# A quantile stage on selection networks: min and max in place with one operand copied to PSUM, two tiles in turn, five gather buffers

## The chip, the cores and the metric

The kernel runs on one core of a Trainium2 chip. The metric is the device time of one execution in microseconds, as the median over several runs. A profiled execution gives, beside its own time, a record of each instruction; engine names are PE (TensorE), PEld (its weight loads), DVE (VectorE), ACT (ScalarE), POOL (GpSimd) and SP (SyncE).

## The reference

Two layers follow each other on a graph of 4096 nodes with 128 features; about 32 neighbours a node.

```python
# layer 0: graph attention, 8 heads
e = leaky_relu(f1[:, :, None] + f2[:, None, :], 0.2)      # f1, f2: nodes @ W[h] @ a1[h], a2[h]
att = softmax(where(adj > 0, e, -9e15), axis=-1)
h = elu(einsum('hnm,hmd->hnd', att, Wh))
x = layernorm(nodes + elu(cat(h) @ W1 + b1)) * gamma + beta
# layer 1: quantiles over the kept neighbours, per feature
rank = cumsum(mask, axis=1) - 1
keep = mask & ~((rank + 1) % skip[:, None] == 0)          # skip = ceil(neighbours / 2), or 1
svals = sort(where(keep[:, :, None], x[None], big), axis=1)
agg = mean of svals at ceil(q * n_keep) - 1 for q in (0.25, 0.5, 0.75)   # 0 with nothing kept
out = (0.5 * agg + 0.5 * x) @ W.T + b + x
```

So each node needs, for each of 128 features, three order statistics over some 10 to 60 values that lie in rows of the first layer's output.

## The kernel before, in words

**Tiles.** 128 nodes make a tile (one node a partition), 32 tiles in all. The nodes are sorted by their number of neighbours (rank_by_count, L593), so that tile t holds nodes with at most CAP[t] neighbours and its list of kept neighbours has 2 * HT[t] slots: 22 in the smallest tile, 42 in the second largest, 62 in the largest (LMAX); 1022 slots in all tiles.

**Attention.** neighbours (L476) finds each node's neighbour list from the adjacency rows, in three blocks of 2, 8 and 22 tiles. The loop at L344 works through each block: it scatters the records (list, number, own index, attention terms, features) into a DRAM table in sorted order, and then takes a step (L311) for each tile. A step fetches the tile's record (fetch_rows, L685: tile R, six buffers, loaded by four DMAs on SP's queue; POOL then gathers one neighbour of each node per indirect DMA into G), writes the finished x1 rows of an earlier pair of tiles with scatter (L168, on POOL; it reads its row numbers from R, so R is held until then), weighs the tile before (weigh_rows, L746) and starts transform (L833) for each pair of tiles. In the first two blocks the order on DVE, PE and ACT is the order of the text (manual_schedule); in the last block a scheduler orders the instructions. In the last block 32 further scatters write list, number and own index of all nodes into all_d, spread over the 22 steps.

**The seam.** After the last step kept_rows (L962) loads all_d and makes, tile by tile with six small DVE instructions each, the slot lists idx; it also counts nodes that the fast way can't take (bad, total). Pads stand in for missing slots: rows of -BIG and BIG in x1_d.

**Quantiles.** The loop at L402 goes over the tiles, small ones first, large ones in the middle. fetch_list (L389) issues one indirect DMA for each slot (gather, L159, on POOL: 128 rows of 512 bytes from x1_d into vals[:, j, :]) and one for the node's own row, xs. vals has two buffers. slot_weights (L1005) makes the weight of each slot in the mean, five small DVE instructions a tile. quantile_out (L1029) runs the selection network (selection_network, L84): 15 or 21 stages a tile. In a stage of distance d the lower of slots i and i + d goes to slot i (mins) and the higher to slot i + d (maxs), where either is needed later. groups (L110) turns the slots of a stage into strided pieces, one DVE tensor_tensor each (L1037), reading the buffer of the stage before and writing the other of two work buffers; slots that no pair touches are copied across by ACT (L1044). Then three to fourteen slots are summed with their weights (L1050), PE transposes the sum (L1056) and multiplies it with the layer's weights (L1060), and DVE adds xb (L1062); POOL scatters the tile to the output (L403, through L168). [...] The scheduler puts the instructions of this stage in order.

## Time and profile before

| | us |
|---|---|
| three runs | 4443.7, 4440.7, 4423.36 |
| median | 4440.7 |
| the profiled execution's own time | 4429.16 |
| its span, first to last instruction | 4427.4 |
| busy: DVE, POOL, ACT, PE | 2559.9, 2815.6, 902.0, 881.4 |
| last gather of the attention stage starts | 2407.0 |
| last x1 rows scattered | 2455.0 |
| first gather of a list, first min of a network | 2458.1, 2509.9 |
| last gather of a list | 4381.5 |
| last DVE instruction (o, L1062) | 4421.6 |

The profile's page gives busy time for each engine, and in 40 equal slices of the span its share in tenths (one slice is 110.7 us). A row of a group reads: line, engine, operation, output<-inputs by name, shapes, count | busy us in all, mean ns of one | idle us of the engine just before them, and what ended the idle time ("issue" is time in which the engine waited for nothing that the profile shows). A row in order of time reads: start us, length us, engine, line, operation, names, shapes, count, and the idle time before it. In the rows names are shortened: x_d is x1_d, xt_d the table of node rows.

### The profile page before, as it was taken

What the parts mean: (1) busy time and instruction counts of PE and PEld (TensorE: products, weight loads), DVE (VectorE), ACT (ScalarE), POOL (GpSimd) and SP (SyncE); (2) the same over time, 40 slices, a digit from 0 to 9 for tenths busy, and PEclk for the clock granted to TensorE, in tenths of its full rate; (3) what the DMA queues carried; (4) which work ended last, traced back from release to release, by engine and by line L of the source; (5) the groups of instructions that cost most, each with busy time, mean ns of one, the idle gap of its engine ahead of it and who ended that gap; (6) DMA issues with size and microseconds to landing.
All of it is one profiled execution on the core that took longest, in us unless ns stands there. A gap on an engine that the chain in (4) does not pass through costs nothing. (4 is left out here: it accounts for less than half of the span.)

```text
span 4427.4 us, 19351 instructions
## 1 busy us (share of the span) xinstructions
PE 881.4 (20%) x4003; PEld 459.4 (10%) x4009; DVE 2559.9 (58%) x5054; ACT 902.0 (20%) x1210; POOL 2815.6 (64%) x2399
## 2 busy tenths in 40 slices
PE   4323444433123332323323000000000000000000
PEld 2000211211122211212212000000000000000000
DVE  5554555555312111112112489987788898779998
ACT  2101212111001110001101022213443223441223
POOL 2432343344566666666664658888888888888885
PEclk9955655556556555555555555555555555555555
DMA  5313233221111111111112101111111101111110
GB/s 169 107 47 114 97 94 102 93 91 44 47 48 48 48 45 48 48 49 49 49 47 56 41 28 40 38 39 41 38 37 33 30 27 33 38 39 38 38 40 29
DMA packets 116271, 242.31 MB, mean 55 GB/s; under 512 B 51920, under 2 KB 69328, under 8 KB 107952
## 3 DMA queue, kind: packets, MB, share of 16 engines
q0 software_dynamic: 76224, 161.01, 13.2%
q10 hardware_dynamic: 12160, 68.49, 4.4%
q1 hardware_dynamic: 27760, 11.49, 1.2%
q14 instruction: 94, 0.77, 0.1%
q8 instruction: 33, 0.54, 0.0%
HBM read 229.64 MB, written 11.18 MB: 54 GB/s over the span
## 5 line engine op out<-in xcount | busy, mean ns | idle before, releaser
L159 POOL DMA_INDIRECT vals<-x_d,idx x1022 | 1474.7, 1443 | 314.1 <-issue 303.1
L1037 DVE TENSOR_TENSOR work<-work 128x256 f32<-128x256 f32 (+12 forms) x1331 | 1497.7, 1170 | 163.0 <-ACT work L1044 126.9
L159 POOL DMA_INDIRECT G<-xt_d,idx x1092 | 1058.1, 969 | 797.0 <-issue 394.6
L1044 ACT COPY work<-work 128x512 f32<-128x512 f32 (+12 forms) x671 | 529.5, 830 | 1102.8 <-DVE work L1037 974.1
L518 DVE MAX8 first<-key 128x8 f32<-128x128 f32 x1024 | 224.3, 286 | 326.6 <-remote 200.3
L1056 PE MATMUL st_ps<-ident,s 128*128 128x128 f32 x32 | 15.2, 474 | 1914.9 <-DVE s L1050 1573.1
L777 PE MATMUL y<-G,pf 128*32 128x129 f32 (+2 forms) x2224 | 219.5, 382 | 454.2 <-issue 345.4
L846 DVE TENSOR_SCALAR e<-e 128x512 f32<-128x512 f32 x64 | 27.7, 433 | 438.5 <-issue 246.1
L512 PE MATMUL key<-sgn,markb 128*128 128x512 bf16 x252 | 146.5, 581 | 531.1 <-DVE first L518 357.5
L798 DVE TENSOR_SCALAR rden<-y 128x6 f32<-128x6 f32 x64 | 7.3, 153 | 354.2 <-remote 179.2
L1056 PEld LDWEIGHTS st_ps<-ident,s 128*128 128x128 f32 x32 | 5.8, 181 | 1924.5 <-DVE s L1050 1581.3
L826 ACT COPY yT<-turned 128x512 f32<-128x512 f32 x64 | 65.5, 1023 | 651.8 <-PE turned L825 335.2
L491 ACT ACTIVATE sgn<-adj_t 128x2048 bf16<-128x2048 int32 x64 | 121.9, 1905 | 372.5 <-PE key L512 174.6
L777 PEld LDWEIGHTS y<-G,pf 128*32 128x32 f32 (+2 forms) x2224 | 138.1, 162 | 539.8 <-issue 408.0
L865 PE MATMUL hT<-yT,W_sb 128*128 128x256 f32 x256 | 119.3, 605 | 276.1 <-DVE hv L848 105.9
L873 ACT ACTIVATE e<-hT 128x512 f32<-128x512 f32 x64 | 38.2, 596 | 610.7 <-remote 438.1
L168 POOL DMA_INDIRECT x_d<-x,R x32 | 32.5, 1016 | 201.4 <-DVE x L912 148.0
L514 PE MATMUL key<-parts,oneb 64*128 64x512 bf16 x256 | 147.4, 576 | 3.2 <-issue 3.2
L168 POOL DMA_INDIRECT rec_d<-rec,ranks x32 | 32.2, 1005 | 159.3 <-issue 123.9
L525 DVE MAX8 rec<-first 128x8 f32<-128x256 f32 x256 | 109.4, 427 | 41.5 <-remote 27.6
L765 DVE TENSOR_TENSOR pf<-z,own 128x1024 f32<-128x1024 f32 x62 | 75.3, 1219 | 94.1 <-ACT z L761 40.5
L1037 DVE TENSOR_TENSOR work<-vals 128x1536 f32<-128x1536 f32 (+8 forms) x64 | 94.9, 1483 | 49.3 <-DMA vals<-x_d,idx 49.0
(171 smaller groups left out, 1674.5 us busy)
## 6 DMA issues: line engine op xcount, KB each, us to landing
adj_t<-in_adj_dram ACTq DMA_DIRECT2D x64, 1024.0 KB
G<-xt_d,idx POOLq DMA_INDIRECT x1092
vals<-x_d,idx POOLq DMA_INDIRECT x1022
R<-rec_d SPq DMA_DIRECT2D x128, 26.4 KB
xt_d<-rec SPq DMA_DIRECT2D x4, 548.0 KB
score<-rec_d SPq DMA_DIRECT2D x132, 1.0 KB
rec<-in_x_dram SPq DMA_DIRECT2D x4, 512.0 KB
Gs<-xt_d,idx POOLq DMA_INDIRECT x92
```

The lines of the kernel that those rows point to most:

```text
L159: nc.gpsimd.indirect_dma_start(out=dst, out_offset=None, in_=rows, in_offset=bass.IndirectOffsetOnAxis(ap=idx, axis=0),)
L491: nc.scalar.activation(sgn, adj_t, AF.Sign, accum_out=cnt[:, i : i + 1])
L512: nc.tensor.matmul(key, lhsT=markb, rhs=sgn[:, ts(b, 512)], start=True, stop=False)
L514: nc.tensor.matmul(key, lhsT=oneb[0:64, :], rhs=parts[:, c0 : c0 + 512], start=False, stop=True)
L518: nc.vector.max(first[:, ts(c0 // CW + c, 8)], key[:, ts(c, CW)])
L525: nc.vector.max(top, first)
L765: nc.vector.tensor_tensor(pf.rearrange("p (g k h) -> p g k h", g=w, k=k), z.unsqueeze(2).to_broadcast(spread), own[w].unsqueeze(1).unsquee ...
L777: nc.tensor.matmul(block(b)[p0 : p0 + m, :], lhsT=pf[:, c : c + m], rhs=G[:, g, 0 : D + 1], start=(i == 0 and b % 3 == 0), stop=last, skip ...
L826: nc.scalar.copy(yT[:, :, ts(place, P)].rearrange("p h (u g) -> p g u h", u=4)[:, ts(half, 16)], t_ps.rearrange("p b (g u h) -> p (b g) u ...
L865: nc.tensor.matmul(hT[:, ts(j, n)], lhsT=consts["W_sb"][:, h, :], rhs=yT[:, h, 0:n], start=True, stop=True,)
L1037: nc.vector.tensor_tensor(slots_of(nxt, (b + low, k, stride, m)), slots_of(cur, (b, k, stride, m)), slots_of(cur, (b + d, k, stride, m)), op,)
L1044: nc.scalar.copy(slots_of(nxt, g), slots_of(cur, g))
```

## The change

It has five parts.

1. **In place, one operand in PSUM.** The work buffers go. A stage splits its slots into three kinds: both ends needed, only the lower, only the higher. Each kind's pieces are cut to at most TURN = 12 slots (pieces_of). For each piece ACT copies the lower slots to a PSUM tile (low, two buffers of 12 * 128 values), and DVE then writes min into the lower and max into the higher slots of vals itself, reading the copy and the higher slots. Pieces of under four slots with only one end are done without a copy. Slots that no pair touches stay where they are.
2. **Two tiles in turn.** quantile_out is a generator that yields after each stage and each step of the end; the loop runs two of them in turn. The order on DVE, PE, ACT and POOL in this part is that of the text.
3. **Five gather buffers.** vals has five buffers of LMOST = 42 slots; the one tile of 62 slots has a buffer of its own (most). Five lists are fetched ahead; when a tile is done its result is scattered, the next list is fetched, and the next tile begins.
4. **Lists and weights for eight tiles at a time.** kept_rows makes its lists with instructions over eight tiles and 62 slots; limits (LOW, CAP, HT for each tile) is filled by POOL at the start. It and slot_places move into step 11 of the last attention block; for that, the 32 scatters to all_d go out four a step in the first eight steps. slot_weights is made the same way, ahead of the quantile loop. Counting bad nodes is now count_bad, after the last step.
5. **Record buffers.** R in fetch_rows has five buffers in place of six.

```diff
--- before.py
+++ after.py
@@ -16,6 +16,7 @@
 PSUM = bass.MemoryType.PSUM
 DRAM = bass.MemoryType.DRAM
 ORDERED = {mybir.EngineType.DVE, mybir.EngineType.PE, mybir.EngineType.Activation}
+ALL = ORDERED | {mybir.EngineType.Pool}
 
 P = 128
 N = 4096
@@ -60,6 +61,8 @@
 ]
 HT = [(c - 1) // 2 for c in CAP]
 LMAX = 2 * max(HT)
+LMOST = 2 * sorted(HT)[-2]
+TURN = 12
 
 
 R_NUM, R_OWN, R_F1 = L, L + 1, L + 2
@@ -127,6 +130,29 @@
                 j += 1
         out.append((b, j - i, stride, n))
         i = j
+    return out
+
+
+def pieces_of(g):
+
+
+    b, k, stride, n = g
+    if k == 1:
+        parts = -(-n // TURN)
+        out = []
+        for i in range(parts):
+            m = (n - sum(p[3] for p in out)) // (parts - i)
+            out.append((b, 1, m, m))
+            b += m
+        return out
+    if n >= TURN:
+        return [p for i in range(k) for p in pieces_of((b + i * stride, 1, n, n))]
+    parts = -(-k // (TURN // n))
+    out = []
+    for i in range(parts):
+        kk = (k - sum(p[1] for p in out)) // (parts - i)
+        out.append((b, kk, stride, n))
+        b += kk * stride
     return out
 
 
@@ -262,6 +288,12 @@
         narrow.append(sets)
     idx = const.tile([P, NT, L], I32, name="idx")
     own_i = const.tile([P, NT], I32, name="own_i")
+    picks = const.tile([P, 4, NT], F32, name="picks")
+    limits = const.tile([P, 3, NT], F32, name="limits")
+    for i, values in enumerate((LOW, CAP, HT)):
+        for t, v in enumerate(values):
+            if t == 0 or v != values[t - 1]:
+                nc.gpsimd.memset(limits[:, i, t:], float(v))
 
 
     rp = tc.alloc_tile_pool(name="recp", bufs=1)
@@ -353,10 +385,17 @@
             adjp.release()
             cp = tc.alloc_tile_pool(name="cnt_all", bufs=2, side="right", reuse_waits="tile")
             ranks = rank_by_count(tc, cp, kp, num, jp1, before, oneb, 0, NT)
+            waiting = list(range(NT))
             for i in range(n):
                 step((recs_d[b], i, CAPS[n][i], t0 + i))
-                for t in range(i * NT // n, (i + 1) * NT // n):
+                for t in waiting[:4]:
                     scatter(nc, all_d, rec[:, t, 0:REC1], ranks[:, t : t + 1])
+                waiting = waiting[4:]
+                if i == n // 2:
+                    R = cp.tile([P, NT, REC1], F32, name="R", bufs=1)
+                    nc.sync.dma_start(R, all_d.rearrange("(t p) w -> p t w", p=P))
+                    kept_rows(tc, cp, R, jp1, pidx, idx, own_i, bad, limits)
+                    slot_places(tc, cp, R, picks, limits)
         else:
             pieces = search(t0 + n, BLOCKS[b + 1])
             quota = -(-BLOCKS[b + 1] * PIECES // n)
@@ -368,9 +407,7 @@
         t0 += n
     for _ in range(3):
         step()
-    R = cp.tile([P, NT, REC1], F32, name="R", bufs=1)
-    nc.sync.dma_start(R, all_d.rearrange("(t p) w -> p t w", p=P))
-    kept_rows(tc, cp, kp, R, jp1, pidx, ones, idx, own_i, bad, total)
+    count_bad(tc, cp, kp, bad, ones, total)
     cp.release()
     attp.release()
     rp.release()
@@ -380,38 +417,51 @@
 
     order = sorted(range(NT), key=lambda t: HT[t])
     order = order[0::2] + order[1::2][::-1]
-    with tc.tile_pool(name="late", bufs=1) as lp, tc.tile_pool(name="sort", bufs=2) as sp, tc.tile_pool(
+    with tc.tile_pool(name="late", bufs=1) as late, tc.tile_pool(name="sort", bufs=5) as sp, tc.tile_pool(
         name="fin", bufs=3
-    ) as fp, tc.tile_pool(name="fin_ps", bufs=2, space=PSUM) as pp:
-        lists = []
-        outs = []
-
-        def fetch_list(t):
-            vals = sp.tile([P, LMAX, D], F32, name="vals")
-            for j in range(2 * HT[t]):
+    ) as fp, tc.tile_pool(name="low_ps", bufs=2, space=PSUM) as lp, tc.tile_pool(
+        name="fin_ps", bufs=1, space=PSUM
+    ) as pp, tc.manual_schedule(engines=ALL):
+        wt = late.tile([P, NT, LMAX], F32, name="wt")
+        slot_weights(tc, late, jp1, picks, wt)
+        waiting = list(order)
+        lists, running, outs = [], [], []
+
+        def fetch_list():
+            t = waiting.pop(0)
+            n = 2 * HT[t]
+            if n > LMOST:
+                vals = sp.tile([P, LMAX, D], F32, name="most", bufs=1)
+            else:
+                vals = sp.tile([P, LMOST, D], F32, name="vals")
+            for j in range(n):
                 gather(nc, vals[:, j, :], x1_d, idx[:, t, j : j + 1])
-            xs = fp.tile([P, D], F32, name="xs")
+            xs = fp.tile([P, D], F32, name="xs", bufs=6)
             gather(nc, xs, x1_d, own_i[:, t : t + 1])
             lists.append((t, vals, xs))
 
-        def write_out():
-            t, o = outs.pop(0)
-            scatter(nc, out, o, own_i[:, t : t + 1])
-
-        wt = lp.tile([P, NT, L], F32, name="wt")
-        for t in order:
-            fetch_list(t)
-            if t == order[0]:
-                R = lp.tile([P, NT, REC1], F32, name="R")
-                nc.sync.dma_start(R, all_d.rearrange("(t p) w -> p t w", p=P))
-                slot_weights(tc, lp, R, jp1, wt)
-            if len(outs) > 1:
-                write_out()
-            if len(lists) > 1:
-                outs.append(quantile_out(tc, sp, fp, pp, *lists.pop(0), wt, ident, WlT, vecs[:, 3, :]))
-        outs.append(quantile_out(tc, sp, fp, pp, *lists.pop(0), wt, ident, WlT, vecs[:, 3, :]))
-        while outs:
-            write_out()
+        def begin():
+            if lists:
+                running.append(
+                    quantile_out(
+                        tc, lp, fp, pp, *lists.pop(0), wt, ident, WlT, vecs[:, 3, :], outs
+                    )
+                )
+
+        for _ in range(5):
+            fetch_list()
+        begin()
+        begin()
+        while running:
+            for g in list(running):
+                if next(g, True):
+                    running.remove(g)
+                    while outs:
+                        t, o = outs.pop(0)
+                        scatter(nc, out, o, own_i[:, t : t + 1])
+                    if waiting:
+                        fetch_list()
+                    begin()
 
 
     flag = nc.values_load(total[0:1, 0:1], min_val=0, max_val=1 << 20)
@@ -686,7 +736,7 @@
 
     nc = tc.nc
 
-    R = ap.tile([P, REC], F32, name="R", bufs=6)
+    R = ap.tile([P, REC], F32, name="R", bufs=5)
     rows = rec_d[ts(i, P), :]
     for u, v in enumerate(rows.rearrange("(g u) w -> u g w", u=4)[k] for k in range(4)):
         nc.sync.dma_start(R[ts(u, 32), :], v)
@@ -959,21 +1009,9 @@
     return keeps, h
 
 
...
+def count_bad(tc, cp, pp, bad, ones, total):
+
+    nc = tc.nc
     t_ps = pp.tile([P, 512], F32, name="key")
     nb = bad.rearrange("p a t -> p (a t)")
     nc.tensor.matmul(t_ps[0:1, 0 : 5 * NT], lhsT=ones[:, 0:1], rhs=nb, start=True, stop=True)
@@ -981,86 +1019,130 @@
     nc.vector.tensor_reduce(tot, t_ps[0:1, 0 : 5 * NT], AX.X, ALU.add)
     nc.vector.tensor_copy(total, tot)
 
+
+def kept_rows(tc, cp, R, jp1, pidx, idx, own_i, bad, limits):
+
+
+    nc = tc.nc
+    num = R[:, :, R_NUM]
+    nc.vector.tensor_copy(own_i, R.bitcast(I32)[:, :, R_OWN])
+    keeps, h = kept_halves(tc, cp, num, NT)
+    few = cp.tile([P, NT], F32, name="few")
+    nc.vector.tensor_tensor(few, num, limits[:, 0, :], ALU.is_lt)
+    nc.vector.tensor_tensor(few, few, keeps, ALU.mult)
+    many = cp.tile([P, NT], F32, name="many")
+    nc.vector.tensor_tensor(many, num, limits[:, 1, :], ALU.is_gt)
+    nc.vector.tensor_tensor(bad[:, 1, :], few, many, ALU.add)
+
     nk = cp.tile([P, NT], F32, name="nk")
     nc.vector.tensor_scalar(nk, h, 2.0, None, ALU.mult)
+    top = cp.tile([P, NT], F32, name="top")
+    nc.vector.tensor_tensor(top, h, limits[:, 2, :], ALU.add)
     padrow = cp.tile([P, 1], F32, name="padrow")
     nc.vector.tensor_scalar(padrow, pidx, float(N), None, ALU.add)
...
+    m = 8
+    big = [P, m, LMAX]
+    jb = jp1[:, 0:LMAX].unsqueeze(1).to_broadcast(big)
+    for t0 in range(0, NT, m):
+        here = slice(t0, t0 + m)
+        pad = cp.tile(big, F32, name="pad", bufs=1)
+        nc.vector.tensor_tensor(pad, jb, top[:, here].unsqueeze(2).to_broadcast(big), ALU.is_gt)
+        nc.vector.tensor_scalar(pad, pad, float(P), padrow, ALU.mult, ALU.add)
+
+        d = cp.tile(big, F32, name="d", bufs=1)
+        nc.vector.tensor_tensor(d, R.bitcast(I32)[:, here, 0:LMAX], pad, ALU.subtract)
+        own = cp.tile(big, F32, name="held", bufs=1)
+        nc.vector.tensor_tensor(own, jb, nk[:, here].unsqueeze(2).to_broadcast(big), ALU.is_le)
+        nc.vector.tensor_tensor(d, d, own, ALU.mult)
+        nc.vector.tensor_tensor(idx[:, here, 0:LMAX], d, pad, ALU.add)
+
+
+def slot_places(tc, pool, R, picks, limits):
 
     nc = tc.nc
     keeps, h = kept_halves(tc, pool, R[:, :, R_NUM], NT)
     nk = pool.tile([P, NT], F32, name="nk")
     nc.vector.tensor_scalar(nk, h, 2.0, None, ALU.mult)
...
+    nc.vector.tensor_scalar(picks[:, 3, :], keeps, 1.0 / 6.0, None, ALU.mult)
     for q in range(3):
...
+        k = picks[:, q, :]
         nc.vector.tensor_tensor(k, places(tc, pool, nk, q + 1), h, ALU.subtract)
...
+        nc.vector.tensor_tensor(k, k, limits[:, 2, :], ALU.add)
+
+
+def slot_weights(tc, pool, jp1, picks, wt):
+
+    nc = tc.nc
+    m = 8
+    big = [P, m, LMAX]
+    jb = jp1[:, 0:LMAX].unsqueeze(1).to_broadcast(big)
+    hit = pool.tile(big, F32, name="hit")
+    for t0 in range(0, NT, m):
+        here = slice(t0, t0 + m)
+        w = wt[:, here, :]
+        for q in range(3):
+            nc.vector.tensor_tensor(
+                hit if q else w,
+                jb,
+                picks[:, q, here].unsqueeze(2).to_broadcast(big),
+                ALU.is_equal,
+            )
+            if q:
+                nc.vector.tensor_tensor(w, w, hit, ALU.add)
+        nc.vector.tensor_tensor(
+            w, w, picks[:, 3, here].unsqueeze(2).to_broadcast(big), ALU.mult
+        )
+
+
+def quantile_out(tc, lp, fp, pp, t, vals, xs, wt, ident, WlT, bl_b, outs):
+
 
     nc = tc.nc
     targets = sorted(quantile_slots(t))
...
+    for d, mins, maxs, _ in selection_network(2 * HT[t], targets):
+        lows, highs = set(mins), set(maxs)
+        kinds = (
+            (sorted(lows & highs), (0, d)),
+            (sorted(lows - highs), (0,)),
+            (sorted(highs - lows), (d,)),
+        )
+        for slots, ends in kinds:
+            for g in (p for whole in groups(slots) for p in pieces_of(whole)):
+                b, k, stride, m = g
+                low, high = slots_of(vals, g), slots_of(vals, (b + d, k, stride, m))
+                if k * m >= 4 or len(ends) == 2:
+                    kept = lp.tile([P, TURN * D], F32, name="low")[:, 0 : k * m * D]
+                    if k > 1:
+                        kept = kept.rearrange("p (k d) -> p k d", k=k)
+                    nc.scalar.copy(kept, low)
+                else:
+                    kept = low
+                for end in ends:
+                    nc.vector.tensor_tensor(
+                        high if end else low, kept, high, ALU.max if end else ALU.min
+                    )
+        yield
 
     s = fp.tile([P, D], F32, name="s")
     nc.scalar.mul(s, xs, 0.5)
+    xb = fp.tile([P, D], F32, name="xb")
+    nc.vector.tensor_tensor(xb, xs, bl_b, ALU.add)
     for j in targets:
         nc.vector.scalar_tensor_tensor(
...
+            s, vals[:, j, :], wt[:, t, j : j + 1], s, ALU.mult, ALU.add
+        )
+    yield
     st_ps = pp.tile([P, P], F32, name="st_ps")
     nc.tensor.transpose(st_ps, s, ident)
     sT = fp.tile([P, P], F32, name="sT")
     nc.scalar.copy(sT, st_ps)
+    yield
     o_ps = pp.tile([P, D], F32, name="fo_ps")
     nc.tensor.matmul(o_ps, lhsT=sT, rhs=WlT, start=True, stop=True)
+    yield
     o = fp.tile([P, D], F32, name="o")
     nc.vector.tensor_tensor(o, o_ps, xb, ALU.add)
...
+    outs.append((t, o))
 
 
 def general_attention(tc, x, adj, wa, x1_d, f2T_d, consts):
```

Where lines are left out, they are the lines of kept_rows, slot_weights and quantile_out that stand in the kernel before.

## The prediction

> **What bounds the kernel now.** I read the page's slices first, then the sums over four stretches of the last stage, then the groups, then single instructions in order of time. From slice 23 on there is only one stage left, the quantile stage, and in it two engines are nearly full:
>
> ```profile
> DVE  5554555555312111112112489987788898779998
> ...
> POOL 2432343344566666666664658888888888888885
> ```
>
> The sums over stretches give, for each engine, busy us and the number of instructions (the order is PE, PEld, DVE, ACT, POOL):
>
> ```profile
> 2600.00:4380.00 1780.00, 36.78 (x87) 19.75 (x87) 1568.86 (x1595) 558.34 (x711) 1475.46 (x1000) 0.50 0.13 37
> ```
>
> POOL issues 1000 indirect DMAs in 1780 us. Each has 0.30 us of issue ahead of it (see the gather rows below), so POOL is taken for 1475 + 300 = 1775 of 1780 us. VectorE is busy for 1569, 88%. So POOL's gathers set the pace here, at 1.78 us each, and VectorE is second. The groups and the gather's spread:
>
> ```profile
> L159 POOL DMA_INDIRECT vals<-x_d,idx x1022 | 1474.7, 1443 | 314.1 <-issue 303.1
> L1037 DVE TENSOR_TENSOR work<-work 128x256 f32<-128x256 f32 (+12 forms) x1331 | 1497.7, 1170 | 163.0 <-ACT work L1044 126.9
> L159 POOL DMA_INDIRECT G<-xt_d,idx x1092 | 1058.1, 969 | 797.0 <-issue 394.6
> ```
>
> ```profile
> L159 POOL DMA_INDIRECT vals<-x_d,idx x1022: 938/1356/4030, 2458.1 to 4381.5; - x171
> ```
>
> The same instruction with rows of the same size takes 969 ns in the attention stage and 1443 here, between 938 and 4030. In order of time it is seen why: it is short while VectorE stands still, and grows while VectorE runs min and max.
>
> ```profile
> 3061.23 0.94 POOL L159 DMA_INDIRECT vals<-x_d,idx  x1 [0.30 <-issue]
> 3062.47 0.94 POOL L159 DMA_INDIRECT vals<-x_d,idx  x1 [0.30 <-issue]
> 3063.71 9.40 DVE L1037 TENSOR_TENSOR work<-work 128x1280 f32<-128x1280 f32 x5 [2.74 <-ACT work L1044]
> ...
> 3067.77 1.83 POOL L159 DMA_INDIRECT vals<-x_d,idx  x1 [0.30 <-DMA vals<-x_d,idx]
> 3069.90 1.63 POOL L159 DMA_INDIRECT vals<-x_d,idx  x1 [0.30 <-issue]
> ...
> 3071.83 2.09 POOL L159 DMA_INDIRECT vals<-x_d,idx  x1 [0.30 <-issue]
> ```
>
> [...] 0.94 us beside an idle VectorE, 1.6 to 2.1 us beside min and max. [...] 692 ns with a PSUM input, 688 without. [...]
>
> ```profile
> L848 DVE TENSOR_TENSOR hv<-hT,e 128x512 f32<-128x512 f32 x8 | 5.5, 692 | 0.4
> L1037 DVE TENSOR_TENSOR work<-work 128x512 f32<-128x512 f32 x88 | 58.6, 688 | 3.5 <-ACT work L1044 1.6
> L1037 DVE TENSOR_TENSOR work<-work 128x2048 f32<-128x2048 f32 x144 | 325.3, 2289 | 33.7 <-ACT work L1044 24.7 <-issue 2.4 <-DVE s L1050 1.5
> L1044 ACT COPY work<-work 128x1024 f32<-128x1024 f32 x124 | 128.2, 1044 | 214.6 <-DVE work L1037 201.5 <-DVE s L1050 7.2 <-issue 4.8
> ```
>
> **The change, part by part.** *Min and max in place.* I counted by evaluating the code's own plan of the network (selection_network, groups, pieces_of) for the 32 tiles. Before: 552 stages, 1395 min and max instructions (the page's 1331 + 64) over 10,766 slots, and 699 ScalarE copies. After: the same 10,766 slots, but in pieces of at most 12 slots: 1823 instructions, of which 348 (675 slots) have both inputs in SBUF because they are not worth a copy; and 761 copies of 5149 slots. From 512 and 2048 elements, an instruction is 0.157 us + 1.042 ns an element. 10,766 x 128 elements are 1436 us either way; the fixed part grows from 219 to 286 us. So 1722 us instead of 1655. But instructions overlap: 1331 x 1.170 = 1557 us of durations fill 1498 us. Where nothing is waited for, a 1.22 us instruction is followed after 1.14 us (2596.09, next at 2597.23), so 0.083 less. A third of them do wait now, mostly for the stage before on the same tile. With two tiles taken stage by stage in turn that stage lies a whole stage back, so I take the overlap for all: 1722 - 1823 x 0.083 = 1571 us.
>
> *Copies to PSUM.* From 512 (616 ns) and 1024 (1044): 0.19 us + 0.836 ns an element, 761 copies = 694 us. They lie beside VectorE, which has 1571. With two PSUM buffers a copy can start when the piece two back has been used. I walked the pieces in program order with these durations and 0.1 us to pass a finished piece on. VectorE then stands still for 60 us in all, nearly all where a small piece is followed by one of 12 slots (a copy of 1.47 us against about 0.5 us of min and max). If the cover of the second tile were gone, the same walk gives 270.
>
> *POOL.* 1022 + 32 + 32 issues x (0.94 + 0.30) = 1347 us. A few grow beside the 348 SBUF pairs and the 140 weighted sums; at 1.30 + 0.10 each it is still 1520. POOL then is no longer the bound. Five buffers let it stay up to three tiles ahead; a finished tile's scatter stands in POOL's order before the next list, and the lists behind it are then already there.
>
> *Weighted sums and the rest.* 140 x 0.377 (four took 1.51 us) = 53 us, now in a row without other work between; xb and o, 64 x 0.2 = 13 us.
>
> *Lists and weights eight tiles at a time.* The 288 small instructions of the lists and the 160 of the weights go; the lists move into step 11 of the last block, where VectorE is under 20% busy. There the 24 wide ones cost 24 x 0.67 = 16 us, plus one 1 MB load on SP's queue ahead of later record loads (the same load takes 11 us today); both lie under some 57 us a tile of POOL time. The weights (24 instructions, 16 us) run while the first lists arrive. What is saved at the seam: little. The last transform's chain ran on through the list work, and the first gather waited for the scatter:
>
> ```profile
> 2450.98 0.96 POOL L168 DMA_INDIRECT x_d<-x,R  x1 [37.68 <-DVE pad L994]
> 2455.05 0.95 POOL L168 DMA_INDIRECT x_d<-x,R  x1 [3.11 <-DVE d L998]
> 2458.13 0.97 POOL L159 DMA_INDIRECT vals<-x_d,idx  x1 [2.13 <-DMA x_d<-x,R]
> ```
>
> I take 5 us, so the first gather at 2453. The 55 memsets of limits at the start are POOL work of 0.1 us beside a load that is waited for anyway: 0.
>
> *Record buffers, six to five.* A record tile is freed by its scatter, and the load follows it at once, 66 us ahead of its use:
>
> ```profile
> 2051.89 1.00 POOL L168 DMA_INDIRECT x_d<-x,R  x1 [0.30 <-issue]
> 2054.16 15.01 SPq L692 DMA_DIRECT2D R<-rec_d  x8
> ```
>
> That is about one tile of POOL time. With one buffer less every second tile loses that lead, and then scatter, load and transpose (some 7 us) stand open in POOL's order, ahead of all later gathers: 16 x 7 = 112 us at the worst. POOL already waits 105 us for PE's y in this stretch, and the two waits may fall together: 0 at best, I take 25.
>
> **Sum, against the profiled execution (span 4427.4, time 4429.2).** First gather 2453; first list 23 x 1.24 + 2.1 = 31 us; the second tile's list 31 us more, of which 2 are used: VectorE is fed from 2513. Then 1571 + 53 + 13 + 60 = 1697 → 4210; last transposes 3, scatter and end 6 → 4219; records 25 → 4244, time 4246. That is 0.9586 of 4429.2. The median of before is 4440.7, 0.3% higher than the profiled one; on it, **4257 us**. VectorE is what is late next: the stage ends with it 97% full.
>
> **Rivals.**
> 1. *VectorE is not so dense.* The overlap is lost where the max writes what the min has just read[...]: 714 pairs x 0.18 = 130[...] us. About 4340 to 4400, still faster. For it: a third of today's instructions start 20 to 120 ns late. Against: independent ones don't. 20%.
> 2. [...] POOL stays the bound at 1.78 us: 2453 + 1086 x 1.78 = 4386, the last list's work 35, end 6: 4427, about 4440 on the median. No change. Against: rows 3061 to 3072. 7%.
> 3. *Slower: copy and min/max take turns.* In place, a copy reads the tile that VectorE is writing. If the order is kept for whole spans of the tile and not for the slots, each copy waits for the min and max of the piece before, and VectorE for each copy: 694 us + 761 x 0.12 = 785 us on VectorE. Then 4244 + 725 = 4970. It decides from about 230 of the 761 copies exposed. Against: a copy of ten slots of vals ran at 2480, with the first tile's gathers still coming (23 issues from 2458), so slots are told apart. 7%.
>
> **Chances.** My forecast, 4200 to 4340, has 66%. A measurement tells this kernel from no change at about 0.5%. Faster by more: 66 + 20 = 86%; within 0.5%: 7%; slower: 7%. Range 4195 to 4400, below for a tighter handshake and no loss on records, above for rival 1 with both its costs.
>
> **What would show it.** Right: gathers of vals near 0.95 us, POOL idle between lists, VectorE over 95% busy from 2515 on with some 1820 min and max, ScalarE's copies near 690 us. Wrong: gathers still at 1.4 us (rival 2); VectorE waiting for ScalarE's copies for hundreds of us (rival 3); VectorE at durations over 0.157 us + 1.04 ns an element, or starts later than the end before (rival 1); POOL waiting for record loads in the attention stage (records over 25 us).

## The result, and the profile after

The changed kernel takes 4567.0 us (median of 4 runs, 4564.2 to 4572.5) beside 4434.2 for the kernel before (a fourth run, 4427.6, joined the three with the median 4440.7): ratio 1.030, 95% interval 1.027 to 1.033. Forecast were 4257 us, 0.959. The change is slower by 3.0%.

Runs come in rounds, each with its own runs of the kernel before, and since these took 4408 to 4438 us (medians) in the round of the result and those of the first eleven experiments but 3943 to 3944 in the later ones, each ratio is taken within its round.

First the slices of the changed kernel's page, then its groups, then the tile view of the list buffers (duration min/median/max in ns, first and last start).

```profile
DVE  5554466546031122211111156888897999999998
...
POOL 2433434443765555555654476566576342445640
```

```profile
L185 POOL DMA_INDIRECT G<-xt_d,idx x1092 | 1050.8, 962 | 955.7 <-issue 505.4
L1121 DVE TENSOR_TENSOR vals<-low,vals 128x1024 f32<-128x1024 f32 (+10 forms) x1359 | 1390.2, 1056 | 211.7 <-remote 65.6
L185 POOL DMA_INDIRECT vals<-x_d,idx x960 | 907.1, 945 | 294.4 <-issue 283.1
...
L827 PE MATMUL y<-G,pf 128*32 128x129 f32 (+2 forms) x2224 | 216.3, 369 | 836.1 <-issue 691.3
...
L194 POOL DMA_INDIRECT out_dram<-o,own_i x32 | 31.8, 993 | 617.5 <-DVE o L1144 607.3
```

```profile
L185 POOL DMA_INDIRECT vals<-x_d,idx x960: 940/944/1213, 2593.5 to 4427.0; - x192
```

What the change is meant to do, it does: list gathers fall from 1443 to 945 ns, and POOL, full in this stage before, now waits 607 us for VectorE's outputs. Yet the first list gather starts at 2593.5 instead of 2458.1, and from there to the end it takes 1970.9 us (4564.4 less 2593.5) where it took 1969.3. So there are two losses to explain: 135 us ahead of the stage that was rebuilt, and a gain inside that stage that didn't come.

Two other lines stand out beside those of before. TensorE's wait ahead of the y matmuls, put down to "issue" (nothing in the trace was waited for), is 691 us; before it was 345. And 66 us of VectorE's waits ahead of min and max are named "remote" (a release from nowhere in the trace). The kernel before has such waits too, but nearly all ahead of its quantile stage; of its page:

```profile
L777 PE MATMUL y<-G,pf 128*32 128x129 f32 (+2 forms) x2224 | 219.5, 382 | 454.2 <-issue 345.4
L798 DVE TENSOR_SCALAR rden<-y 128x6 f32<-128x6 f32 x64 | 7.3, 153 | 354.2 <-remote 179.2
```

Both waits belong together, as two stretches of the changed kernel in order of time show. First the attention stage:

```profile
2129.74 1.00 POOL L194 DMA_INDIRECT x_d<-x,R  x1 [0.30 <-issue]
2132.07 8.51 SPq L742 DMA_DIRECT2D R<-rec_d  x8
...
2133.61 0.38 PE L827 MATMUL y<-G,pf 128*32 128x129 f32 x1 [2.42 <-issue]
2135.01 0.13 PEld L827 LDWEIGHTS y<-G,pf 128*32 128x32 f32 x1 [2.67 <-issue]
...
2148.02 0.23 DVE L848 TENSOR_SCALAR rden<-y 128x6 f32<-128x6 f32 x2 [64.45 <-PE y L827]
...
2168.59 0.14 DVE L756 TENSOR_SCALAR bad<-R 128x1 f32<-128x1 f32 x1
...
2168.94 0.20 DVE L771 STREAM_TRANSPOSE idx<-list 128x32 int32<-128x32 int32 x1
...
2169.63 0.97 POOL L185 DMA_INDIRECT G<-xt_d,idx  x1 [36.37 <-PE y L827]
```

The scatter frees a record buffer, and the load follows at 2132. VectorE first touches the new record at 2168.59: its order has the last tile's rden, yn and transform ahead of it, and these stood 64 us behind matmuls that TensorE started one in 2.8 us. POOL can't form the next gathers until then: the trace puts its wait down to y, but the first gather starts 0.49 us after VectorE has transposed the row numbers (idx), here as at four other long pauses of POOL. Now the quantile stage:

```profile
3443.04 0.28 DVE L1121 TENSOR_TENSOR vals<-low,vals 128x128 f32<-128x128 f32 x1
...
3443.63 0.27 ACT L1117 COPY low<-vals 128x128 f32<-128x128 f32 x1 [5.33 <-DVE vals L1121]
...
3451.33 0.29 DVE L1121 TENSOR_TENSOR vals<-low,vals 128x128 f32<-128x128 f32 x1 [8.01 <-remote]
```

The copy is over at 3443.90, its reader starts 7.4 us later, and in between POOL issues a gather every 1.25 us. I call both *hold-ups*: instructions that start late with nothing in the trace to wait for. TensorE's slow matmuls start most often 2.8 us apart, also 0.7, 1.4, 2.1 and 3.5; VectorE is up to 8 us late. In the changed kernel's quantile stage, behind the second list, 63 of the 70 us in VectorE's gaps over 2 us lie inside POOL's bursts of gathers or start within 8 us behind one; but the bursts with these 8 us cover three quarters of that time, so this alone proves little. In the last block, TensorE's slow steps end 6 to 11 us after POOL's last DMA ahead of each long pause.

### The profile page after: what moved, and what is told of

Its sections match the earlier page's. It is cut to its first block, busy times and chain, and to the rows that moved or that the text cites. A ratio compares the mean times of both kernels' runs of the same rounds, so it can differ in the third digit from the quotient of the medians.

```text
span 4564.4 us, 19103 instructions
## 1 busy us (share of the span) xinstructions
PE 841.6 (18%) x4003; PEld 441.7 (10%) x4009; DVE 2585.1 (57%) x5090; ACT 996.2 (22%) x1272; POOL 2279.8 (50%) x2453
## 5 line engine op out<-in xcount | busy, mean ns | idle before, releaser
L1121 DVE TENSOR_TENSOR vals<-low,vals 128x1024 f32<-128x1024 f32 (+10 forms) x1359 | 1390.2, 1056 | 211.7 <-remote 65.6
L185 POOL DMA_INDIRECT vals<-x_d,idx x960 | 907.1, 945 | 294.4 <-issue 283.1
L1117 ACT COPY low<-vals 128x1024 f32<-128x1024 f32 (+9 forms) x701 | 610.0, 877 | 1047.4 <-DVE vals L1121 643.9
L194 POOL DMA_INDIRECT out_dram<-o,own_i x32 | 31.8, 993 | 617.5 <-DVE o L1144 607.3
L809 DVE TENSOR_TENSOR z<-G,f1x 128x256 f32<-128x256 f32 (+3 forms) x46 | 22.0, 477 | 336.0 <-DMA G<-xt_d,idx 328.0
L1121 DVE TENSOR_TENSOR most<-low,most 128x1024 f32<-128x1024 f32 (+7 forms) x116 | 132.1, 1166 | 2.5 <-issue 0.2
L915 PE MATMUL hT<-yT,W_sb 128*128 128x256 f32 x256 | 105.8, 554 | 102.4 <-DVE hv L898 43.1
L1121 DVE TENSOR_TENSOR vals<-vals 128x256 f32<-128x256 f32 (+2 forms) x335 | 116.2, 408 | 5.3 <-DVE vals L1121 3.3
```

The source lines that it names most:

```text
L185: nc.gpsimd.indirect_dma_start(out=dst, out_offset=None, in_=rows, in_offset=bass.IndirectOffsetOnAxis(ap=idx, axis=0),)
L194: return nc.gpsimd.indirect_dma_start(out=rows, out_offset=bass.IndirectOffsetOnAxis(ap=idx, axis=0), in_=src, in_offset=None,)
L915: nc.tensor.matmul(hT[:, ts(j, n)], lhsT=consts["W_sb"][:, h, :], rhs=yT[:, h, 0:n], start=True, stop=True,)
L1117: nc.scalar.copy(kept, low)
L1121: nc.vector.tensor_tensor(high if end else low, kept, high, ALU.max if end else ALU.min)
```

## Experiments

**Theories.** *Records*: the fifth record buffer alone costs the 135 us. *Order*: a max right behind its own min in place starts late. *Narrow ends*: both tiles reach their narrow last stages together. *Hold-ups*: POOL's back-to-back indirect DMAs hold up the other engines, and both losses are mostly this.

Where VectorE's time in the quantile stage goes is told by one sum: from the arrival of the second list to its last instruction, durations less overlap, plus gaps under 0.1 us, plus idle (gaps of 0.1 us and over). (The "213 us of idle" in the expectations count the 29 us wait for the second list itself; behind it there are 184.)

| | sum | durations | overlap | short gaps | idle |
|---|---|---|---|---|---|
| forecast | 1697 | 1788 | -151 | 0 | 60 |
| changed | 1901 | 1778 | -88 | 27 | 184 |
| half a tile apart | 1942 | 1765 | -86 | 26 | 237 |
| mins then maxs | 1885 | 1780 | -118 | 13 | 211 |
| low in SBUF | 1830 | 1785 | -88 | 29 | 104 |
| gathers left out | 1775 | 1780 | -91 | 29 | 57 |
| gathers spaced | 1828 | 1780 | -89 | 28 | 108 |
| changed, round of 3944 | 1777 | 1781 | -90 | 30 | 57 |
| six and twos, round of 3943 | 1757 | 1782 | -125 | 14 | 86 |

### The records and the lists

```diff
-    R = ap.tile([P, REC], F32, name="R", bufs=5)
+    R = ap.tile([P, REC], F32, name="R", bufs=6)
```

The edit also moves limits into the last block's pool, where VectorE fills it instead of POOL; so it is in all runs with six record buffers.

> The changed kernel with six record buffers again; the limits (384 bytes a partition) move into the pool of the last block, so that they fit. Record theory: the 135 us by which the first list gather came later (2593.5 against 2458.1) are all from the fifth buffer: first gather at 2450 to 2470, gaps of POOL ahead of every second tile back from 24-41 us to 10-19, time 4425 to 4445. Rival, the lists in step 11 and the four scatters a step disturb the order of the last block: first gather stays past 2570, time over 4540.

4445.0 us, ratio 1.002 (1.000 to 1.003); the first list gather as the record theory says:

```profile
L185 POOL DMA_INDIRECT vals<-x_d,idx x960: 940/944/1350, 2467.2 to 4302.4; - x192
```

From 1400 us on, POOL pauses for at most 20 us ahead of gathers, where the changed kernel pauses for 24 to 41: with six buffers the row numbers are mostly ready 40 us and more ahead, and POOL waits for y.

The other way round, in the kernel before (bufs=6 to 5):

> The kernel before with five record buffers instead of six and nothing else. Record theory: first list gather at about 2590, time about 4565 to 4575 (plus 130). Rival: first gather within 20 us of 2458, time 4435 to 4460.

4545.8 us, ratio 1.025 (1.024 to 1.027); first list gather at 2601.6, 143 us later, of which the end keeps 107 (130 were expected). Both sides agree: here the one buffer is worth 107 us or more.

```diff
-                if i == n // 2:
-                    R = cp.tile([P, NT, REC1], F32, name="R", bufs=1)
-                    ...
-                    slot_places(tc, cp, R, picks, limits)
...
     for _ in range(3):
         step()
+    R = cp.tile([P, NT, REC1], F32, name="R", bufs=1)
+    ...
+    slot_places(tc, cp, R, picks, limits)
     count_bad(tc, cp, kp, bad, ones, total)
```

> The changed kernel with the list work and its 1 MB load back behind the last step; five record buffers stay. Record theory: first list gather at 2595 to 2625, time 4570 to 4600. Rival, the lists in step 11 are what delays the last block: first gather before 2510, time under 4485.

4570.7 us, ratio 1.030 (1.029 to 1.032); first gather 2596.5. Where the lists are made matters by 3 us.

### The quantile stage

```diff
         begin()
+        for _ in range(len(list(selection_network(2 * HT[order[0]], sorted(quantile_slots(order[0]))))) // 2):
+            next(running[0])
         begin()
```

> The changed kernel, the second tile begun when the first is half through its stages, so that the narrow last stages of one lie beside wide ones of the other. Theory that the 212 us of VectorE idle behind the second list come mostly from both tiles being narrow together and both starting late: idle under 120 us, time 4455 to 4490. Rival, the idle is from stages of the machine (the waits named remote and issue) and from handing over at any width: idle stays near 200, time 4550 to 4570.

4602.4 us, ratio 1.038 (1.036 to 1.040). A miss for the theory of narrow ends, and slower than its rival's numbers too: idle rose to 237 us. The theory falls.

```diff
+        for a in range(0, len(parts), 2):
+            made = []
+            for g, ends in parts[a : a + 2]:
...
-                for end in ends:
-                    nc.vector.tensor_tensor(
-                        high if end else low, kept, high, ALU.max if end else ALU.min
-                    )
+                made.append((low, kept, high, ends))
+            for i in range(2):
+                for low, kept, high, ends in made:
+                    for end in ends[i : i + 1]:
+                        nc.vector.tensor_tensor(
+                            high if end else low, kept, high, ALU.max if end else ALU.min
+                        )
```

> The changed kernel with the order of one stage's min and max turned: pieces taken in twos, both min first and then both max, so that for 460 of the 714 pieces with both ends the max no longer follows its own min directly. Theory that a max right behind its min starts 34 ns after its end, where others start 82 ns before it, because it writes what the min reads: 460 x 0.117 = 54 us less, time 4505 to 4525. Rival, the gap belongs to the PSUM buffer shared by the two (both read the same copy) or to the form: gaps stay, time 4555 to 4580; it is also slower if the copies no longer fit beside.

4548.0 us, ratio 1.027 (1.023 to 1.030), between the two expectations. The order is what matters: starts about 34 ns late fall from 663 to 244 of 1822, and overlap and short gaps give 44 us. But idle takes 27 of them back: waits for copies rise from 12 to 32 us and those named issue from 19 to 46. That two PSUM buffers are too few for the copies is likely: with pieces in twos and four buffers, in SBUF (a run below), these waits are 0.4 us.

This run doesn't tell whether a max is late because it writes what its min reads or because both read the same inputs. The traces do. In the kernel before 366 max stand right behind the min of the same inputs and write elsewhere: all start some 84 ns before its end. In the changed kernel all 714 that stand behind their own min wait for a semaphore that VectorE itself raises (365 of those 366 don't), and where nothing else delays them they start 34 ns after the min's end. With the lows in SBUF it is the same (overlap -88 us and short gaps 29, where the changed kernel has -88 and 27), so PSUM isn't the cause.

> Three edits together: six record buffers (limits in the last block's pool), pieces in twos, and the first tile three stages ahead of the second. If they add: 4445 - 54 - 15 = 4376, range 4365 to 4395, 1.0 to 1.7% under the kernel before. If the time that the twos free is lost again in waits for copies, 4425 to 4450.

The three edits together: 4435.8 us, ratio 1.000 (0.999 to 1.002). They don't add: VectorE is idle for 231 us behind the second list.

```diff
-            for j in range(n):
-                gather(nc, vals[:, j, :], x1_d, idx[:, t, j : j + 1])
+            for a in range(0, n, n // 2):
+                rows = x1_d[0 : P * (n // 2), :].rearrange("(p j) d -> p j d", p=P)
+                nc.sync.dma_start(vals[:, a : a + n // 2, :], rows)
```

> The changed kernel with the quantile stage's 1022 list gathers left out: each list is filled by two plain loads of as many rows, in order and not by index, on SP's queue, so the output isn't the reference's. Attention stage as it is. Theory that VectorE and ScalarE stand still in bursts of GpSimd's indirect DMAs (165 of the 213 us of idle over 0.1 us lie in them): idle behind the second list under 100 us, time 4385 to 4430, of which some 40 are the earlier lists. Rival, the idle is the hand-over between ScalarE and VectorE at narrow stages: idle stays over 150, time 4480 to 4535.

4394.7 us, ratio 0.992 (0.988 to 0.995), within the hold-up theory's numbers. Over the whole stage VectorE is idle for 72 us in gaps over 0.1 us; waits named remote are gone:

```profile
DVE o L1145 <- PE fo_ps L1142: 32.1, 32, 1.1
DVE vals L1122 <- ACT low L1118: 23.6, 59, 0.7
DVE vals L1122 <- DMA vals<-x_d: 15.6, 2, 13.2
```

Behind the second list its sum is 1775 us, 57 of them idle.

```diff
-    ) as fp, tc.tile_pool(name="low_ps", bufs=2, space=PSUM) as lp, tc.tile_pool(
+    ) as fp, tc.tile_pool(name="low_sb", bufs=2) as lp, tc.tile_pool(
```

> The changed kernel with the copies of the low ends in two SBUF buffers of the same size instead of PSUM. [...] nearly all min and max have two SBUF inputs again, gathers of vals go back from 0.945 to 1.4 us or more, POOL loses its 600 us of idle, VectorE's durations stay; time 4550 to 4620. Rival, the short gather is not from PSUM but from the spacing of the gathers: gathers stay under 1.05 us, time 4560 to 4575.

4498.6 us, ratio 1.016 (1.012 to 1.019): faster than the changed kernel, which neither theory expected. The gathers went back up, though not all the way to 1.4 us:

```profile
L185 POOL DMA_INDIRECT vals<-x_d,idx x960 | 1202.7, 1253 | 294.4 <-issue 283.5 <-DMA vals<-x_d,idx 7.3 <-DMA x_d<-x,R 2.1
```

1253 ns instead of 945 beside min and max with both inputs in SBUF; in the kernel before, whose min and max also read SBUF alone, it was 1443. VectorE's durations hardly moved (1060 ns beside 1056). But gathers now stood 1.40 us apart (median) instead of 1.25, and VectorE lost 80 us of idle. So slower gathers helped; next, gathers that are only spaced, with the lows in PSUM:

```diff
+        spare = late.tile([P, 192], F32, name="spare")
...
             for j in range(n):
                 gather(nc, vals[:, j, :], x1_d, idx[:, t, j : j + 1])
+                nc.gpsimd.memset(spare, 0.0)
```

> The changed kernel with one memset of 192 elements a partition on GpSimd behind every list gather of the quantile stage; lows stay in PSUM. The gathers then start 1.5 to 1.6 us apart instead of 1.24, about as in the run with the lows in SBUF (1.55). Rate theory: gathers 1.24 us apart hold up the other engines' instructions, gathers 1.55 us apart do not; VectorE's idle behind the second list falls from 213 to 110-150 us, the waits named remote from 65 to under 15, and the time to 4485-4515 although GpSimd does more work. Rival, it was the place of the low ends in SBUF that helped (PSUM reads wait for something): remote stays at 50 to 70, time 4565 to 4590.

4491.4 us, ratio 1.019 (1.015 to 1.023). Of this run, VectorE's waits and the added work:

```profile
DVE vals L1124 <- remote: 3.8, 3, 1.8
```

```profile
L441 POOL MEMSET spare<- 128x192 f32 x1022 | 280.4, 274 | 7.7 <-remote 4.5 <-issue 1.4 <-POOL spare L441 0.3
```

Gathers 1.39 us apart (median) instead of 1.25 take the remote waits ahead of min and max from 65.6 to 3.8 us, and 280 us of useless work on POOL make the kernel faster. That is the hold-up theory, and the place of the lows is not the reason. The round isn't either: the next run, of the same round and with the lows in SBUF, has 102 us of idle behind the second list, where the earlier round had 104. The hold-ups are not gone, though: remote waits ahead of the weighted sums rose from 8.5 to 22.0 us, and idle is 108 us, not 57. The gap between gathers was smaller than I had expected (1.5 to 1.6): the memset took the place of nearly half of the 0.30 us of issue.

> Six record buffers (limits in the last block's pool) and the low ends in SBUF. If the two gains add: 4445 - 68 = 4377, range 4365 to 4390, 1.2 to 1.5% under the kernel before. If the longer gathers make lists late: 4400 to 4430.

4342.2 us, ratio 0.985 (0.981 to 0.988). The gains add, as a ratio; the time lies below the expected one because the kernel before, too, took only 4408 in this round.

> The same, with pieces in twos (both min, then both max) and four SBUF buffers for the low ends instead of two, so that copies need not wait for the max. Expected 54 us under the run without twos if the freed time is kept: 4320 to 4345. If [...] the copies still come late: 4355 to 4380.

4341.9 us, ratio 0.984 (0.981 to 0.988). The time is in the first range by luck of the round; against the run without twos (4342.2) they gave nothing. From the second list on, VectorE waits 167 us for lists instead of 67, likely because it now slows POOL (gathers at 1377 ns instead of 1253).

> Six record buffers, low ends in PSUM, spaced list gathers, pieces in twos. In the run with the lows in SBUF the twos gave nothing, since VectorE then waited 167 us for lists from a GpSimd that it held up itself; here GpSimd's gathers are not held up. If that was the reason: lists are not late, ratio to the kernel before 0.972 to 0.981. Rival, two PSUM buffers are too few for pieces in twos and VectorE waits for copies instead: over 60 us of waits for ScalarE's copies, ratio 0.983 to 0.990.

3842.9 us, ratio 0.974 (0.972 to 0.976). The ratio is as hoped, but this was the first round of the lower level, so it doesn't settle what it was made for. It opened a larger question instead.

### The same kernels without hold-ups

In the rounds with 3944 us the traces hardly show such hold-ups. The kernel before, run there for its trace: first the tile view, then the group of y.

> The kernel before as it is, for a trace in a round in which it takes about 3944 us. Hold-up theory: the attention stage alone is what the hold-ups lengthened; first list gather at 2000 to 2015 instead of 2458, TensorE's waits named issue ahead of y under 30 us instead of 345; quantile stage still paced by POOL's gathers at 1.7 to 1.8 us, 1925 to 1945 us long. Rival, the quantile stage is shorter too: under 1900.

```profile
L159 POOL DMA_INDIRECT vals<-x_d,idx x1022: 940/1358/4022, 1991.0 to 3896.4; - x171
```

```profile
L777 PE MATMUL y<-G,pf 128*32 128x129 f32 (+2 forms) x2224 | 156.8, 387 | 559.0 <-DVE pf L765 558.5 <-DVE yn L809 0.5
```

3944.4 us. No wait for issue ahead of y, the attention stage is 467 us shorter, the quantile stage 18: the gathers paced it either way. (First gather and stage are 9 and 6 us outside the expected numbers.) Up to POOL's first gather the two levels run alike: it starts at 95.6 us there and 96.2 here. From 100 to 200 us POOL then issues 39 indirect DMAs there and 62 here. Then the changed kernel and the variants (edits as above), in one round:

> The changed kernel as it is, beside the kernel before. If this round is one in which the kernel before takes about 3944 us (as in the run of the six-spaced-twos kernel, where TensorE's matmuls of y no longer wait 1.4 us each for issue): hold-up theory says that both losses shrink with the hold-ups, first gather within 30 us of the six-record kernel's, VectorE's idle behind the second list under 130 us, ratio 0.97 to 1.00. Rival, the fifth record buffer and the idle cost the same without hold-ups: ratio 1.02 to 1.04. In a round in which the kernel before takes about 4430: ratio 1.027 to 1.033 again, which tells nothing new.

> Six record buffers, all else as changed. Round of about 3944: hold-up theory, within 30 us of the changed kernel; rival, about 120 us less than the changed kernel. Round of about 4430: ratio 1.000 to 1.003.

> Six record buffers and low ends in SBUF. Round of about 3944: hold-up theory, no gain over low ends in PSUM, within 20 us of the six-record kernel, since there are no hold-ups to avoid; rival, SBUF is better in itself, 60 to 80 us less. Round of about 4430: ratio 0.982 to 0.988.

> Six record buffers, spaced gathers, pieces in twos, low ends in PSUM. Round of about 3944: ratio 0.972 to 0.976 again. Round of about 4430: 0.972 to 0.984 if the spacing ends the hold-ups and the twos gain 20 to 50 us more; 0.985 to 0.990 if waits for copies take the gain.

| | us | ratio (95%) | first gather | from there to the end |
|---|---|---|---|---|
| before (traced one round later) | 3944.3 | 1 | 1991.0 | 1951.4 |
| changed | 3873.3 | 0.982 (0.980 to 0.984) | 2025.5 | 1846.4 |
| six records | 3851.2 | 0.976 (0.974 to 0.978) | 2005.3 | 1846.7 |
| six, low in SBUF | 3907.8 | 0.990 (0.989 to 0.992) | 2005.1 | 1901.9 |
| six, spaced, twos | 3845.4 | 0.975 (0.973 to 0.976) | 2005.8 | 1839.1 |

Here the changed kernel is 1.8% *faster*. Its tile view and VectorE's largest waits in the quantile stage:

```profile
L185 POOL DMA_INDIRECT vals<-x_d,idx x960: 940/944/2919, 2025.5 to 3734.7; - x192
```

```profile
DVE vals L1121 <- DMA vals<-x_d,idx: 65.6, 2, 36.4
DVE o L1144 <- PE fo_ps L1141: 30.2, 30, 1.1
DVE vals L1121 <- ACT low L1117: 23.6, 59, 0.7
```

No remote, no issue; and VectorE's sum behind the second list, 1777 us, is that of the run without list gathers, 1775, part for part. The fifth buffer costs 20 us of first gather, not 126. In the last 18 tiles a record's load is used 3 to 7 us after it starts; with hold-ups it lay 24 to 45 us. And the lows in SBUF now *lose* 57 us against PSUM, which neither expectation had: VectorE waits 111 us for lists instead of 66. What was a remedy against hold-ups is a burden without them.

> Six record buffers and pieces in twos, low ends in two PSUM buffers, gathers not spaced. Round of about 3944: the max no longer right behind its min in 460 pieces is worth 54 us against the six-record kernel's 3851 if waits for copies stay near 24 us: 3797 to 3815. If the two PSUM buffers make the copies late: 3825 to 3845. Round of about 4430: 4420 to 4440.

3832.2 us, ratio 0.972 (0.970 to 0.973), the best of this level. Against six records alone (3851.2) the order gave 50 us in overlap and short gaps and lost 30 in idle (waits for copies rose from 24 to 51 us): the case with late copies. The spacing gives nothing here: with it, six records and twos took 3845.4.

## Why the prediction was wrong

Forecast were a span of 4244 and a second list at 2513; it came at 2653.7 (2538 with the records' 25 us). The 320 us between forecast and trace divide so:

- **Counts, durations, copies: right.** 1778 us of VectorE durations against 1722 + 53 + 13 = 1788 (the two lines shown give 0.154 us of fixed part, not 0.157: some 5 of the 10 us); ScalarE's copies 673 against 694. A PSUM source costs no more than an SBUF one (1056 and 1060 ns).
- **Gathers: right.** 945 ns, beside min and max too: 811 of the 960 had these beside them for over 80% of their length and took 945 ns in the mean, where 761 such gathers of the kernel before took 1575 (and 142 with no min or max beside them 945). That lows in PSUM would bring this, no trace of before showed; it was my estimate. POOL idles between lists. Rivals 2 and 3 are out: gathers are short, and VectorE waited 12 us for copies. (Rival 1's 130 us alone would have made 4257 + 130 = 4387, so the 4400 of the range left 13 us for its other cost.)
- **Lists and seam: 5 us saved was wrong**, it is 9 us lost with six records (2467.2) and 14 in the other rounds. I didn't take this apart; the cause is open.
- **Overlap: the step "I take the overlap for all" failed.** 714 max stand right behind the min that reads what they write, wait for it, and start about 34 ns after its end instead of 82 before: 91 us with the short gaps (151 - 88 + 27), of which 714 x 0.117 are 84. It was rival 1's lost overlap; its sign and place were right, its 130 us too many. It is nearly the same with hold-ups and without.
- **"The handshake 60" failed: 184 with hold-ups, 124 us more.** What it lacked was that engines start late while POOL issues gathers. By shortening the gathers the change drew them from 1.67 to 1.25 us apart (medians), and so made its own hold-ups: lows in SBUF or a memset between gathers take 76 to 80 us back, no list gathers 127. Without hold-ups it is 57, and that this is near 60 is partly luck: 24 us of it are waits for copies, for which the 60 stood, and 30 are waits of o for TensorE, which the sum left out.
- **"Records 25" failed with hold-ups (126), and held without (20).** It was a guess between 0 and 112. The 7 us for scatter, load and transpose were right for a VectorE that is free. I took the spare lead for the whole cost and didn't look how late VectorE reached the record in its order: with hold-ups on TensorE, 24 to 45 us after the load's start.

Sum: 101 (records) + 14 (seam) + 91 (order) + 124 (idle) less 10 (durations) = 320. Without hold-ups the same steps give 3777 from the 1991.0 of the kernel before, against a span of 3872, nearly all of it the order (91); so there, too, only 71 of the 165 us forecast were gained. The sign of the result was decided by hold-ups, 225 of 320 us. They were to be seen in the trace of before: 345 us of issue ahead of y, and 354 us of waits ahead of rden behind it. I read the last stage's sums closely and left those lines alone.

**What stays open** is why hold-ups come in some rounds and not in others. The levels followed each other in time: the longer times are those of every round up to the eleventh experiment, the shorter ones those of every later round. The chip's number on record doesn't decide it: rounds at 4408 to 4438 ran on chips 7, 8 and 14 (the round of the result has no number), those at 3943 to 3944 on 14, 2 and 10. Nor are the transfers themselves slower: the packets of the gathers' queue took 586 us on each of the 16 DMA engines (mean) in both traces of the kernel before. Shown is that in the quantile stage VectorE's hold-ups go when the list gathers are left out, and shrink when these are spaced. For TensorE's hold-ups in the attention stage no run took the gathers away; that they come from POOL's bursts rests on where they lie in time. Not shown is what it is that is held up.

## What to carry to other kernels

Before you shorten the pitch of one engine's DMA issues, read what the other engines wait for under "issue" and "remote" while these run: here that idle grew with the rate, and a change priced without it changed its sign. When a buffer is taken away, price it by the time at which the engine that uses it next gets there in the trace, not by the load's own latency. An in-place pair (min, then max onto its input) is worth separating by another instruction: here the order gave 44 to 50 us and cost 27 to 30 in waits, for copies above all, so a further buffer for the copy is worth a try.

## What the runs showed of the hardware

- In the rounds with hold-ups and gathers 1.25 us apart, VectorE's instructions started up to 8 us late, TensorE's small matmuls of y mostly 0.7 to 3.5 us apart in steps of 0.7 where they were slow; at 1.39 us apart VectorE's remote waits ahead of min and max fell from 66 to 4 us, and its idle from 184 to 108; without list gathers it was 57.
- The same kernel took 4408 to 4438 us in some rounds and 3943 to 3944 in others, its attention stage alone 467 us less; TensorE's granted clock hardly differs (0.557 and 0.564 in the two traces).
- A max that waits for the min just before it starts 34 ns after that one's end (median, in the changed kernel); in the kernel before, where only 1 of 366 pairs on the same inputs waits for VectorE itself, the max starts 84 ns before the min's end (median).
- A 192-element memset behind a gather took 274 ns but moved the next gather only 0.14 us.
- ScalarE's copy to PSUM is a little quicker than to SBUF: 877 against 907 ns in the mean of the same 701 copies.
